# Small attention beside a second attention and two feed-forwards: a fifth work tile, one more step between stages, and normalisations tile by tile

## The chip, the cores and the metric

The kernel runs on one core of a Trainium2 chip. The metric is the device time of one execution in microseconds (us). The kernel before takes 4474.51 us, the median of three runs between 4472.06 and 4476.75.

A core has a matrix engine (TensorE, PE in the profile, with weight loads as PEld), three engines for elementwise work (VectorE or DVE, ScalarE or ACT, GpSimd or POOL), and SyncE (SP), which here only issues DMAs. Each engine works through its own queue strictly in order; an instruction that waits for a semaphore holds up all that stands behind it.

## The reference

Eight sequences of 512 tokens with 256 channels, all in float32, go through four blocks with residuals:

```python
x = x + attention_a(layernorm(x))   # per token: 16 heads of 64 channels, a 64 x 64 causal matrix per head
x = x + ffn(layernorm(x))           # 256 -> 1024 gated, two hidden layers 1024 -> 1024, 1024 -> 256
x = x + attention_b(layernorm(x))   # causal over the 512 tokens, 16 heads of 16 channels
x = x + ffn(layernorm(x))           # the same weights again
```

The first attention is unusual. For each token and head, channel q attends to the channels k <= q of the same token: `softmax_k(Q[q]*K[k]/8)` weighs `V[k]`. There is no contraction for the matrix engine in it; it is elementwise work on 64 x 64 outer products. The feed-forward is `silu(x@w1*s1) * (x@w2*s2)`, then twice `gelu(h@w*s)`, then `h@w3*s3`.

## The kernel before, in words

A batch is one sequence, held as four tiles of 128 tokens by 256 channels in SBUF (`self.x[b]`). `AttentionA` computes the first attention; `after_a` is a Python generator which writes the other three blocks of each batch (`ffn`, `attention_b`, `ffn`). The driver at the end of `fast_path` interleaves the two by hand: under `tc.manual_schedule` the queues of PE, DVE, ACT and POOL hold instructions in the order in which the Python code writes them. The first attention is written step by step; after each of the three `yield`s of a step the driver draws as much from `after_a` as keeps `spent`, the sum of what its `yield`s return, in proportion to `total`. A batch's other blocks are thus written while the first attention works on the next batch, and those of the last batch stand alone at the end.

**The first attention.** A group is one tile of tokens and four heads (`GW` = 256 channels), NG = 4 groups per tile, 16 per batch, 128 in all. The causal triangle is cut into squares of 32, 16, 8, 4, 2 and 1 channels, sorted into four units per group (`units`); a step of the pipeline is one unit. A unit lives in a work tile `w` of 128 x 4096 floats from the pool `wt` (four buffers): half for e = exp(q*k), half for e*v. Its stages are

- `scores` (L718): the products q*k, on POOL from an SBUF copy of q (`kt`) for the first two units, on DVE from q in PSUM for the others;
- `exps` (L731) on ACT;
- `weigh` (L742) on DVE: e*v, with v in PSUM; then for the three large units a DMA that POOL issues (L744) and that adds the second half of the tile onto the first, inside SBUF;
- `fold` (L752) on POOL: for the 32-squares one more halving, which waits for that DMA; for the small squares (L757, L779) additions into `acc`;
- `gather` (L773) on DVE: sums over the last eight columns, then POOL adds them to the rows of `acc` (L779);
- `divide`: a DVE reciprocal (L783) and a POOL product (L784), once per group; `turn_group` (L792) and `project_out` (L801) on PE, and the sum with x on DVE (L808).

In step n, `step` writes the scores of unit n, then `weigh(n - 1)` with its DMA, `fold(n - 2)`, `gather(n - 3)`, and last `exps(n)`. `project` (L686, L693) makes k and q|v of a group two steps ahead with weights `wqv`, `wk` from the pool `wp`, which has two buffers; `load_w` fetches the next group's weights on SP.

**Normalisations.** `stats` takes mean and variance on DVE, the square root on ACT (L518), reciprocal and shift on DVE (L519, L524), for several tiles in one go; `normed` applies them on ACT (L532, L536), PE transposes (L543), ACT copies (L544). Before a feed-forward and before the second attention, three tiles are done together (`begin`) and the fourth later (`norm_last`, `finish`).

**The other blocks.** `later(fn)` puts a piece of code off to the next `flush()`. In `ffn`, `gate` writes silu on ACT (L927) and the product on DVE (L928) right after each other, the rounding to fp32r on ACT (L931) and the remainder on POOL (L932) put off. The hidden layers (L1016) read weights of 1 MB each, whose DMAs POOL issues (L855), 20 per batch with the gates'. Blocks for activations come from the pool `hp` with eight buffers, taken in turn.

Of the kernel before, what the change touches and what calls it, by code (L numbers as in the profile page):

```python
# [16 lines left out]
P = 128  # L17
# [267 lines left out]
def fast_path(ctx: ExitStack, tc: tile.TileContext, k, t, flag):  # L285

    nc = tc.nc
    ident, eps = k.ident, k.eps
# [3 lines left out]
    wp = ctx.enter_context(tc.tile_pool(name="wp", bufs=2))  # L292
# [5 lines left out]
    hp = ctx.enter_context(tc.tile_pool(name="hp", bufs=8))  # L298
# [27 lines left out]
    for g in range(NG):  # L326
        if g < 2:

            wqv = wp.tile([P, DC, 2 * GW], F32, tag="wqv", name=f"wqv_0_{g}")
            wk = wp.tile([P, DC, GW], F32, tag="wk", name=f"wk_0_{g}")  # L330
        else:
            both = block(f"fit_{g}")
            wqv = both[:, : DC * 2 * GW].rearrange("p (c f) -> p c f", c=DC)
            wk = both[:, DC * 2 * GW : DC * 3 * GW].rearrange("p (c f) -> p c f", c=DC)
        nc.sync.dma_start(wqv, wqv_r[:, :, g, :])
        nc.sync.dma_start(wk, wk_r[:, :, g * GW : (g + 1) * GW])
        fitted.append((wqv, wk))
# [171 lines left out]
    def stats(b, xt, part, tiles=range(NT)):  # L509

        i0, i1 = tiles[0], tiles[-1] + 1
        mv = small.tile([P, NT, 2], F32, tag=f"mv_{part}", name="mv", bufs=2)[:, i0:i1]
        for i in tiles:
            st = small.tile([P, 6], F32, tag=f"st_{part}", name="st")
            nc.vector.bn_stats(st, xt[:, i, :])
            nc.vector.bn_aggr(mv[:, i - i0, :], st)
        rstd = small.tile([P, NT], F32, tag=f"rstd_{part}", name="rstd", bufs=2)[:, i0:i1]
        nc.scalar.activation(rstd, mv[:, :, 1], AF.Sqrt, bias=eps)  # L518
        nc.vector.reciprocal(rstd, rstd)  # L519
        if part == "f":  # L520
            shift = small.tile([P, NT], F32, tag="shift", name="shift", bufs=2)[:, i0:i1]
        else:
            shift = means[:, b, 0 if part == "a" else 1, i0:i1]
        nc.vector.scalar_tensor_tensor(shift, mv[:, :, 0], -1.0, rstd, ALU.mult, ALU.mult)  # L524
        return {i: (rstd[:, i - i0 : i - i0 + 1], shift[:, i - i0 : i - i0 + 1]) for i in tiles}

    def normed(xi, rn, part):

        rstd, shift = rn
# [9 lines left out]
    def turned_over(dst, xn, pool):  # L539
# [4 lines left out]
        nc.scalar.copy(dst, pt)  # L544
# [4 lines left out]
    units = (((32, 0, 2),), ((32, 2, 2),), ((16, 0, 4),), ((8, 0, 4), (4, 0, 4), (2, 0, 4), (1, 0, 4)))  # L549
    NU = len(units)  # L550

# [10 lines left out]
    def pieces(w, n, off, nsq, cols):  # L562
# [11 lines left out]
        if n < 16:  # L574
            e, ev = (
                w[:, a * 2048 + off : a * 2048 + off + nsq * n * n].rearrange("p (x i j) -> p x i j", i=n, j=n)
# [22 lines left out]
    class AttentionA:  # L599
# [3 lines left out]
        def __init__(self):  # L603
            self.x = {0: x_first}
            self.rn, self.live = {}, {}
            self.w = {(0, g): fitted[g] for g in range(2)}
            self.wo = {}
            self.load_wo(0, 0)
            self.ready = set()
# [3 lines left out]
            self.steps = len(self.todo) + 11  # L613
# [10 lines left out]
        def load_wo(self, b, g):  # L624
            if b < NB:
                wo = wp.tile([P, GW // P, D], F32, tag="wo", name=f"wo_{b}_{g}", bufs=1)
# [6 lines left out]
        def step(self, n):  # L633
            b, i, g, u = self.at(n)
            if b is not None:
                self.scores(b, i, g, u)
            b, i, g, u = self.at(n + 40)
            if u == 0 and g == 0 and i == 0 and b > 0:
                self.x[b] = load_x(b)
            b, i, g, u = self.at(n + 7)  # L640
            if u == 0 and g == 0 and i == 0:
                self.rn[b] = stats(b, self.x[b], "a")
            b, i, g, u = self.at(n + 4)
            if u == 0 and g == 0:
                self.norm(b, i)
            yield
            b, i, g, u = self.at(n - 1)
            if b is not None:
                self.weigh(b, i, g, u)
            b, i, g, u = self.at(n - 2)  # L650
            if b is not None:
                self.fold(b, i, g, u)
            b, i, g, u = self.at(n + 2)
            if u == 0:
                self.project(b, i, g)
            yield
            b, i, g, u = self.at(n - 3)
            if b is not None:
                self.gather(b, i, g, u)

            b, i, g, u = self.at(n - 4)
            if u == NU - 1:
                self.divide(b, i, g)
            b, i, g, u = self.at(n - 8)
            if u == NU - 1:
                self.turn_group(b, i, g)
            b, i, g, u = self.at(n - 9)
            if u == NU - 1:
                self.project_out(b, i, g)
            yield  # L670
            b, i, g, u = self.at(n)
            if b is not None:
                self.exps(b, i, g, u)

        def norm(self, b, i):
            xnt = lnp.tile([P, DC, P], F32, tag="xnt_a", name=f"xnta_{b}_{i}", bufs=NT)
            turned_over(xnt, normed(self.x[b][:, i, :], self.rn[b][i], "a"), ps_a)
            self.live[b, i] = xnt

        def project(self, b, i, g):  # L680
# [8 lines left out]
            kt = ap_.tile([P, 2, GW], F32, tag="k", name=f"k_{u}")  # L689
            nc.scalar.copy(kt[:, 0], pk)  # L690
            qv = ps_qv.tile([P, 2, GW], F32, tag="qv", name=f"qv_{u}")
            for c in range(DC):
# [6 lines left out]
                )  # L699
            nc.scalar.copy(kt[:, 1], qv[:, 0])  # L700
            acc = ap_.tile([P, 2, GW], F32, tag="acc", name=f"acc_{u}", bufs=4)
            self.live[b, i, g] = (qv, kt, acc)
            if i == 1 and (b, g) != (0, 0):
                self.load_w(b + (g + 1) // NG, (g + 1) % NG)

        def scores(self, b, i, g, n_u):

            qv, kt, acc = self.live[b, i, g]
            w = wt.tile([P, 4096], F32, tag="w", name=f"w_{b}_{i}_{g}_{n_u}")
            self.live[b, i, g, n_u] = w  # L710
            if n_u == 0:
                nc.vector.tensor_tensor(acc[:, 0, :], qv[:, 0, :], kt[:, 0], ALU.mult)
            for n, off, nsq, cols in squares(units[n_u]):

                eng, q = (nc.gpsimd, kt[:, 1]) if n_u < 2 else (nc.vector, qv[:, 0])
                for e, ev, rows, columns in pieces(w, n, off, nsq, cols):
# [3 lines left out]
                    )  # L720

        def exps(self, b, i, g, n_u):
            qv, kt, acc = self.live[b, i, g]
            w = self.live[b, i, g, n_u]
            if n_u == 0:
                nc.scalar.activation(acc[:, 0, :], acc[:, 0, :], AF.Exp, scale=C**-0.5)
            if n_u < 3:
                e = w.rearrange("p (b a r) -> p a b r", a=2, b=units[n_u][0][0] // JB)[:, 0]
            else:
                e = w[:, : sum(nsq * n * n for n, off, nsq, cols in squares(units[n_u]))]  # L730
            nc.scalar.activation(e, e, AF.Exp, scale=C**-0.5)  # L731

        def weigh(self, b, i, g, n_u):


            qv, kt, acc = self.live[b, i, g]
            w = self.live[b, i, g, n_u]
            if n_u == 0:
                nc.vector.tensor_tensor(acc[:, 1, :], acc[:, 0, :], qv[:, 1, :], ALU.mult)
# [3 lines left out]
            if n_u < 3:  # L743
                nc.gpsimd.dma_start(w[:, :2048], w[:, 2048:], accum_op=ALU.add)  # L744

        def fold(self, b, i, g, n_u):

            qv, kt, acc = self.live[b, i, g]
            w = self.live[b, i, g, n_u]
            for n, off, nsq, cols in squares(units[n_u]):  # L750
                if n == 32:
                    nc.gpsimd.tensor_tensor(w[:, :1024], w[:, :1024], w[:, 1024:2048], ALU.add)  # L752
                if n <= 2:
                    both = w.rearrange("p (a f) -> p a f", a=2)[:, :, off : off + nsq * n * n]
                    both = both.rearrange("p a (r j) -> p a r j", j=n)
                    if n == 2:
                        nc.gpsimd.tensor_tensor(both[..., :1], both[..., :1], both[..., 1:], ALU.add)  # L757
                    self.add_rows(acc, n, cols, both[..., 0])

        def gather(self, b, i, g, n_u):  # L760

            qv, kt, acc = self.live[b, i, g]
            w = self.live.pop((b, i, g, n_u))
            for n, off, nsq, cols in squares(units[n_u]):
                if n <= 2:
                    continue
                if n >= 16:
                    both = w[:, : 2 * nsq * n * JB].rearrange("p (a r j) -> p a r j", a=2, j=JB)
                else:
# [569 lines left out]
```

## Time and profile before

| | |
|---|---|
| median of the runs | 4474.51 us |
| profiled execution | 4477.29 us, span 4475.5 us |
| granted TensorE clock, mean | 0.806 |
| busy, PE / DVE / ACT / POOL | 66% / 78% / 54% / 66% of the span |
| DMA queues: POOL's, SP's | 56.3%, 6.3% of 16 engines |
| activation table loads on ACT | 408, 1283 ns each |
| work DMA (L744) | 384, 1 MB each, 7.2 us from issue to landing |

How to read it: a group's line names the line of the kernel, engine, operation, output and inputs with shape, count, then busy time, mean ns of one, and the idle time of the engine just before it with what ended that. Busy time leaves out instructions that issue DMAs. A wait is listed as waiter, waited-for, us in total, times, longest.

### The profile page before, as it was taken

How to read it: one execution, taken by the hardware profiler on the slowest of the kernel's cores; microseconds unless marked ns; L12 is line 12 of the kernel's file. 1: busy time of each engine (PE TensorE's matmuls, PEld its weight loads, DVE VectorE, ACT ScalarE, POOL GpSimd, SP SyncE). 2: the span in 40 equal slices, each digit the busy share in tenths (PEclk: the TensorE clock that was granted, in tenths of full speed). 3: DMA queues.
4: the chain of work that ended last, by engine and by line, in shares of the span. 5: the costliest groups of instructions: out<-in, count | busy, mean ns of one | idle time of the engine just before them, and what ended most of it. 6: DMA issues, size and time to landing. Idle time of an engine off the chain costs nothing. (4 is left out here: it accounts for less than half of the span.)

```text
span 4475.5 us, 37073 instructions
## 1 busy us (share of the span) xinstructions
PE 2959.5 (66%) x11880; PEld 2017.9 (45%) x11880; DVE 3511.3 (78%) x4113; ACT 2422.0 (54%) x3068; POOL 2962.6 (66%) x2634
## 2 busy tenths in 40 slices
PE   3322277567865777757875678657777568756998
PEld 2111154245633555335642456335553356425757
DVE  5988877888888888878878788888888788787205
ACT  3333365565754765556654666547655566546332
POOL 6777776766776776767767667667767677676201
PEclk6555588788987889878987889778898789878999
DMA  7555566657755767647765577557676477655514
GB/s 234 124 123 119 123 163 168 124 140 178 192 125 111 181 165 176 134 112 177 178 168 124 139 177 198 119 111 182 161 178 133 110 180 172 168 115 135 180 43 147
DMA packets 118364, 670.24 MB, mean 150 GB/s; under 512 B 12672, under 2 KB 31883, under 8 KB 43536
## 3 DMA queue, kind: packets, MB, share of 16 engines
q0 software_dynamic: 78336, 570.46, 56.3%
q1 hardware_dynamic: 39824, 97.32, 6.3%
q8 instruction: 96, 1.57, 0.1%
q14 instruction: 108, 0.88, 0.1%
HBM read 255.12 MB, written 9.96 MB: 59 GB/s over the span
## 5 line engine op out<-in xcount | busy, mean ns | idle before, releaser
L742 DVE TENSOR_TENSOR w<-w,qv 128x1024 f32<-128x1024 f32 (+3 forms) x1280 | 1198.7, 985 | 443.5 <-ACT w L731 443.5
L731 ACT ACTIVATE w<-w 128x2048 f32<-128x2048 f32 (+1 forms) x512 | 966.0, 1887 | 842.0 <-POOL w L718 560.8
L1016 PE MATMUL ph<-h,hidden 128*128 128x512 f32 x4096 | 1095.3, 424 | 158.4 <-POOL h L932 90.4
L773 DVE TENSOR_REDUCE red<-w 128x128 f32<-128x1024 f32 (+2 forms) x640 | 1036.6, 1636 | 23.9 <-POOL w L752 19.1
L718 POOL TENSOR_TENSOR w<-k 128x1024 f32<-128x1024 f32 x512 | 1036.2, 2136 | 7.6 <-ACT k L700 7.4
L1016 PEld LDWEIGHTS ph<-h,hidden 128*128 128x128 f32 x4096 | 819.7, 203 | 386.9 <-POOL h L932 113.7
L744 POOL DMA_DIRECT2D w<-w x384 | 334.8, 872 | 979.1 <-DVE w L742 331.4
L752 POOL TENSOR_TENSOR w<-w 128x1024 f32<-128x1024 f32 x256 | 664.1, 2594 | 64.6 <-DMA w<-w 64.2
L718 DVE TENSOR_TENSOR w<-qv,k 128x1024 f32<-128x1024 f32 (+3 forms) x768 | 601.5, 838 | 6.9
L779 POOL TENSOR_TENSOR acc<-acc,red 128x256 f32<-128x256 f32 (+1 forms) x640 | 473.1, 739 | 139.5 <-DVE red L773 121.0
L948 PE MATMUL pw<-xnt,gate 128*128 128x512 f32 (+2 forms) x1152 | 328.7, 439 | 166.8 <-ACT silu L927 84.6
L543 PE MATMUL ps_ln<-ident,xn 128*128 128x128 f32 x256 | 76.5, 415 | 488.7 <-ACT xn L536 330.6
L1126 PE MATMUL pyb<-eb,vb 128*32 128x512 f32 (+3 forms) x1024 | 219.6, 525 | 255.7 <-ACT eb L1121 255.5
L948 PEld LDWEIGHTS pw<-xnt,gate 128*128 128x128 f32 x1152 | 236.6, 225 | 244.9 <-ACT silu L927 101.8
L686 PE MATMUL pk<-wk,xnta 128*128 128x256 f32 x512 | 191.6, 512 | 196.6 <-DVE x L808 195.2
L693 PE MATMUL qv<-wqv,xnta 128*128 128x512 f32 x512 | 288.0, 692 | 0.0
L543 PEld LDWEIGHTS ps_ln<-ident,xn 128*128 128x128 f32 x256 | 37.3, 193 | 529.7 <-ACT xn L536 353.7
L1041 PE MATMUL pof<-w,h 128*128 128x256 f32 x1024 | 244.9, 399 | 12.5 <-ACT h L981 12.5
L981 ACT ACTIVATE h<-ph,s_sb 128x512 fp32r<-128x512 f32 (+1 forms) x256 | 172.2, 688 | 129.7 <-PE ph L1016 128.4
L1126 PEld LDWEIGHTS pyb<-eb,vb 128*32 128x32 f32 x1024 | 66.2, 117 | 362.2 <-ACT eb L1121 336.5
L686 PEld LDWEIGHTS pk<-wk,xnta 128*128 128x128 f32 x512 | 124.1, 258 | 231.4 <-DVE x L808 206.3
L1041 PEld LDWEIGHTS pof<-w,h 128*128 128x128 f32 x1024 | 204.4, 202 | 48.0 <-ACT h L981 17.3
(130 smaller groups left out, 4196.5 us busy)
## 6 DMA issues: line engine op xcount, KB each, us to landing
w<-w POOLq DMA_DIRECT2D x384, 1024.0 KB, 7.2
hidden<-in_h POOLq DMA_DIRECT2D x128, 1024.0 KB, 6.6
gate<-in_w12p POOLq DMA_DIRECT2D x32, 1024.0 KB, 5.7
w<-w_d SPq DMA_DIRECT2D x16, 1024.0 KB
wqv<-wqv_d SPq DMA_DIRECT2D x30, 512.0 KB, 3.1
wo<-in_wo SPq DMA_DIRECT2D x32, 256.0 KB, 6.6
wbqk<-wbqk_d SPq DMA_DIRECT2D x8, 1024.0 KB
w<-in_h SPq DMA_DIRECT2D x8, 1024.0 KB, 8.5
```

The lines of the kernel that those rows point to most:

```text
L686: nc.tensor.matmul(pk, xnt[:, c, :], wk[:, c, :], start=(c == 0), stop=(c == DC - 1))
L693: nc.tensor.matmul(qv.rearrange("p j f -> p (j f)"), xnt[:, c, :], wqv[:, c, :], start=(c == 0), stop=(c == DC - 1),)
L718: eng.tensor_tensor(e, rows(q).to_broadcast(shape), columns(kt[:, 0]).to_broadcast(shape), ALU.mult)
L731: nc.scalar.activation(e, e, AF.Exp, scale=C**-0.5)
L742: nc.vector.tensor_tensor(ev, e, columns(qv[:, 1]).to_broadcast(list(e.shape)), ALU.mult)
L744: nc.gpsimd.dma_start(w[:, :2048], w[:, 2048:], accum_op=ALU.add)
L752: nc.gpsimd.tensor_tensor(w[:, :1024], w[:, :1024], w[:, 1024:2048], ALU.add)
L773: nc.vector.tensor_reduce(red, both, AX.X, ALU.add)
L779: nc.gpsimd.tensor_tensor(rows, rows, part.rearrange("p a (x i) -> p a x i", i=n), ALU.add)
L948: nc.tensor.matmul(pj[:, toks], w[:, m % 4, j, c, :], xs[:, p, c, toks], start=(p == 0 and c == 0), stop=(p == 1 and c == DC - 1),)
L1016: nc.tensor.matmul(pss[j], w[:, j, c, :], h_in(p, c), start=(p == 0 and c == 0), stop=(p == 1 and c == MC - 1),)
L1041: nc.tensor.matmul(po, h(0, c)[:, i * P : (i + 1) * P], w3[:, c, :], start=(c == 0), stop=(c == MC - 1))
```

## The change

It has five parts.

1. *The first attention's pipeline.* The units are reordered, 32, 16, 32 and small; POOL does the scores of the first and third. The small unit gets a work tile of its own (`ws`, one buffer, two times 1920 floats), so with the four `w` there are five. `exps` moves to the next step, `weigh` to n - 2, the DMA becomes a stage of its own (`halve`) between the two halves of POOL's scores, `fold` is at n - 3, `gather` at n - 4 (small unit: n - 3), POOL's additions one part after the gather. Projections, copies, transposes and additions to x are split and spread over the steps.
2. *Normalisations.* `stats` becomes `moments` on DVE and `scales` on POOL, with the power -0.5 of variance + eps in place of square root and reciprocal. `Normed` works tile by tile, each link put off to a later `flush`, and the blocks that read it wait (`nx.wait`) until enough tiles are written.
3. *Other blocks.* In `gate` the product is put off by one flush; the additions to x in `attention_b` too.
4. *Buffers.* The pool `wp` has one buffer instead of two, `load_w` comes at the group's last projection; `hp` has seven instead of eight, with hidden activations in pairs of chunks.
5. *The driver.* The loop begins two steps earlier, `total` is 304.8 instead of 299.4, the pipeline is one step shorter at its end; the weights of groups 1 to 3 are fitted during the first steps.

```diff
-    wp = ctx.enter_context(tc.tile_pool(name="wp", bufs=2))
+    wp = ctx.enter_context(tc.tile_pool(name="wp", bufs=1))
...
-    hp = ctx.enter_context(tc.tile_pool(name="hp", bufs=8))
+    hp = ctx.enter_context(tc.tile_pool(name="hp", bufs=7))
...
-        nc.scalar.activation(rstd, mv[:, :, 1], AF.Sqrt, bias=eps)
-        nc.vector.reciprocal(rstd, rstd)
...
-        nc.vector.scalar_tensor_tensor(shift, mv[:, :, 0], -1.0, rstd, ALU.mult, ALU.mult)
...
+    def scales(mv, rstd, shift):
+        nc.gpsimd.tensor_scalar(rstd, mv[:, :, 1], EPS, None, ALU.add)
+        nc.gpsimd.tensor_tensor(rstd, rstd, k.power[:, : rstd.shape[-1]], ALU.pow)
+        nc.gpsimd.tensor_tensor(shift, mv[:, :, 0], rstd, ALU.mult)
+        nc.gpsimd.tensor_scalar(shift, shift, -1.0, None, ALU.mult)
...
-    units = (((32, 0, 2),), ((32, 2, 2),), ((16, 0, 4),), ((8, 0, 4), (4, 0, 4), (2, 0, 4), (1, 0, 4)))
+    units = (((32, 0, 2),), ((16, 0, 4),), ((32, 2, 2),), ((8, 0, 4), (4, 0, 4), (2, 0, 4), (1, 0, 4)))
...
+    SMALL = 1920
...
         def step(self, n):
-            b, i, g, u = self.at(n)
-            if b is not None:
-                self.scores(b, i, g, u)
...
+            before = self.at(n - 2)
+            if before[0] is not None:
+                self.weigh(*before)
+            unit = self.at(n)
+            on_pool = unit[3] in (0, 2)
+            if on_pool:
+                half = self.scores(*unit)
+                next(half)
+            if before[0] is not None:
+                self.halve(*before)
+            if on_pool:
+                next(half, None)
...
+            if self.at(n - 1)[0] is not None:
+                self.exps(*self.at(n - 1))
+            yield
+            if unit[0] is not None and not on_pool:
+                for _ in self.scores(*unit):
+                    pass
+            for args in self.sums:
+                self.add_rows(*args)
+            self.sums = []
+            b, i, g, u = self.at(n - 3)
+            if u in (0, 2):
+                self.fold(b, i, g, u)
...
+            yield
+            b, i, g, u = self.at(n - 4)
+            if u in (0, 1, 2):
+                self.gather(b, i, g, u)
+            b, i, g, u = self.at(n - 3)
+            if u == NU - 1:
+                self.gather(b, i, g, u)
+            b, i, g, u = self.at(n + 3)
+            if u == 0:
+                self.project(b, i, g)
...
-            if i == 1 and (b, g) != (0, 0):
+            if i == NT - 1:
                 self.load_w(b + (g + 1) // NG, (g + 1) % NG)
...
-            w = wt.tile([P, 4096], F32, tag="w", name=f"w_{b}_{i}_{g}_{n_u}")
+            if n_u < NU - 1:
+                w = wt.tile([P, 4096], F32, tag="w", name=f"w_{b}_{i}_{g}_{n_u}")
+            else:
+                w = wt.tile([P, 2 * SMALL], F32, tag="ws", name=f"ws_{b}_{i}_{g}", bufs=1)
...
-                eng, q = (nc.gpsimd, kt[:, 1]) if n_u < 2 else (nc.vector, qv[:, 0])
+            eng, q = (nc.gpsimd, kt[:, 1]) if n_u in (0, 2) else (nc.vector, qv[:, 0])
...
+        def tile(self, i):
+            mv = small.tile([P, 1, 2], F32, tag="mv", name="mv")
...
+            moments(self.xt[:, i, :], mv[:, 0, :])
+            def scale():
+                scales(mv, rstd, shift)
+                later(normalise)
+            def normalise():
+                xn = normed(self.xt[:, i, :], rstd, shift, self.part)
+                later(lambda: turn_tile(xn))
...
+            later(scale)
+
+        def wait(self, tiles):
+            while self.done < tiles:
+                flush()
+                yield 0.8
...
+            def times():
+                nc.vector.scalar_tensor_tensor(x, p2, s_sb[:, 1, m : m + 1], x, ALU.mult, ALU.mult)
+                later(high)
...
-    total = 299.4
+    total = 304.8
...
-        for n in range(-7, a.steps):
+        for n in range(-9, a.steps):
```

## The prediction

> **What bounds the kernel now.** I read the page's totals first, then the waits, then the first attention running alone, then one batch cut at each reciprocal (one per group of four units). The page, and the waits of VectorE:
>
> ```profile
> PE 2959.5 (66%) x11880; PEld 2017.9 (45%) x11880; DVE 3511.3 (78%) x4113; ACT 2422.0 (54%) x3068; POOL 2962.6 (66%) x2634
> ...
> L744 POOL DMA_DIRECT2D w<-w x384 | 334.8, 872 | 979.1 <-DVE w L742 331.4
> ...
> w<-w POOLq DMA_DIRECT2D x384, 1024.0 KB, 7.2
> ```
>
> ```profile
> DVE w L742 <- ACT w L731: 443.5, 143, 6.2
> DVE silu L928 <- ACT silu L927: 158.4, 64, 5.3
> ```
>
> No engine is full. VectorE is the fullest, and it stands mostly before the weighting, waiting for an exponential. GpSimd's 66% leaves out the issuing of DMAs. From about 110 to 545 us the first attention runs alone; VectorE and GpSimd there, in the timeline:
>
> ```profile
> 352.93 0.41 DVE L739 TENSOR_TENSOR acc<-acc,qv 128x256 f32<-128x256 f32 x1
> 356.90 2.35 DVE L742 TENSOR_TENSOR w<-w,qv 128x1024 f32<-128x1024 f32 x2 [3.56 <-ACT w L731]
> ```
>
> ```profile
> 375.20 2.64 POOL L752 TENSOR_TENSOR w<-w 128x1024 f32<-128x1024 f32 x1
> 377.51 0.74 POOL L779 TENSOR_TENSOR acc<-acc,red 128x128 f32<-128x128 f32 x1
> 377.91 1.01 POOL L784 TENSOR_TENSOR acc<-acc 128x256 f32<-128x256 f32 x1
> 378.60 4.13 POOL L718 TENSOR_TENSOR w<-k 128x1024 f32<-128x1024 f32 x2
> ...
> 387.60 0.86 POOL L744 DMA_DIRECT2D w<-w  x1 [0.66 <-DVE w L742]
> 388.21 0.91 POOL L757 TENSOR_TENSOR w<-w 128x256 f32<-128x256 f32 x1
> ```
>
> ```profile
> DMA to landing us min/median/max: 6.9/7.0/7.6
> ```
>
> Reciprocals stand 27.82 us apart (347.28, 375.11, 402.92). VectorE has 24.19 us of work in that, plus one stall of 3.56: GpSimd's scores, the exponential and the weighting follow each other without slack. The last line is the accumulating DMA in this stretch: it lands 7.0 us after its issue, 7.6 at most.
>
> One later batch takes 522.95 us (753.83 to 1276.78), VectorE busy for 433.0. Its groups by stage (us, length, busy PE, PEld, DVE, ACT, POOL, clock, DMA share, GB/s):
>
> ```profile
> 781.67:809.47 27.80, 18.73 (x111) 8.01 (x108) 24.19 (x26) 15.02 (x26) 20.87 (x19) 0.81 0.66 144
> 932.29:976.97 44.68, 32.57 (x107) 24.51 (x107) 32.04 (x45) 32.89 (x37) 32.18 (x30) 0.77 0.57 142
> 1205.33:1237.06 31.73, 29.33 (x121) 22.91 (x120) 24.29 (x26) 18.89 (x19) 20.94 (x19) 0.95 0.92 235
> ```
>
> ```profile
> DMA to landing us min/median/max: 7.0/8.1/12.6
> ```
>
> First, a group beside the second attention's scores: nothing lost against running alone. There are five such, 140.2 us. Second, a group beside a gate; the five at normalisations and gates take 205.4 us, VectorE busy 155.7. Third, a group beside the hidden layers: six, 177.4 us, with DMA engines up to 92% busy; the last line is the accumulating DMA from 1147 to 1237 us, landing in 8.1, at worst 12.6.
>
> **What the Trainium skill says.** "Perfetto Trace Analysis", per-instruction lifecycle: the profiled end of a GpSimd-issued DMA is the end of descriptor generation, not of the data. The trace agrees: 0.87 us of L744 against 7.0 to landing. "DMA: Bandwidth & Descriptors", issuing engines are not separate queues: all DMAs interleave on the same 16 engines. Agreed: the landing grows where weights load. "ScalarE: Activation LUTs", what a table load costs: 1283 ns at each change of set. The trace has exactly that, 1283. "GPSIMD Engine Reference", 3.1: a two-input operation costs GpSimd about twice VectorE's time. Here 128x1024 takes 1.9 to 2.1 us against 1.2.
>
> **The change, part by part.**
>
> *One more step.* The weighting moves from n-1 to n-2, its DMA between the two halves of the scores, the fold to n-3, the gather to n-4; units become 32, 16, 32, small, so that GpSimd's scores (u 0 and 2) alternate with VectorE's. This removes the 3.56 stall: the exponential of u=0 now has the whole next step. VectorE's work stays 24.2. What is late next is GpSimd's fold, which waits for the DMA. GpSimd's queue per group, start to start from the stretch above: scores 4 x 1.91, issues 3 x 0.61, folds 2 x 2.31, small squares 1.00 + 1.74, additions 2 x 0.41 + 0.73 + 1.5, division 0.69: 20.6. In the new order between the DMA of u=2 and its fold lie its own 0.61, half a score 1.91, division 0.69, addition 0.41: 3.6 us; landing in 7.0 leaves a stall of 3.4. For u=0: 0.61 + 1.91 + 0.73 + 0.61 + 0.41 + 1.5 = 5.8, stall 1.2. Before, a fold had a whole step, 7.5 to 8.6 us, and hardly waited. So GpSimd takes 20.6 + 4.6 = 25.2, more than VectorE: about 2.6 us saved per group running alone. Behind the waiting fold are the next scores; their exponential has some 5 us of slack.
>
> *Normalisations.* Square root, reciprocal and shift leave ScalarE and VectorE: about 5 us of VectorE per batch, and 408 table loads become some 304, 104 x 1.283 = 133 us of ScalarE, which isn't full, so nothing directly. GpSimd gets 13 x 4 tiny dependent operations per batch. The trace has no power. An addition of 128x128 costs 0.45 alone, 128x1024 1.95: 0.23 fixed, 0.3 to 0.35 with a dependence. Lower end 4 x 0.3 = 1.2 us per tile; upper end, a power of several us, 6. I take 1.6, as the power must cost something: 12 x 1.6 = 19 us per batch, all in the five normalisation and gate groups. In exchange each link is put off by a flush, so the engines no longer stand in the chain.
>
> *Gate, additions, copies put off.* VectorE's wait for silu (158.4 in all) should mostly go.
>
> *Single buffers of qkv weights.* The load is now issued after the group's last projection, four steps (about 29 us) ahead of need; landings are 3.1 and 6.3 us. Waits ahead of it on SP are for earlier TensorE work. Nothing; uncovered it would cost up to 9 us x 31. Seven hidden blocks instead of eight: each reuse follows a reader that is already done. Nothing; up to 5 us per layer if not. "q and v in PSUM" is what L718 and L742 read already.
>
> *A batch.* Beside scores: landing 7.4 there, GpSimd 26.0 a group, five are 130. Hidden layers: 20.6 + 1.1 other work + 2.7 weight issues x 0.62 + stalls at a landing of 8.1 of 4.5 + 2.3, less 1.8 filled by the added work: 28.3; the DMA engines' own work is about 25 us per group (share x length), 88% of that, so landings will grow: I take 29, six are 174. Normalisations and gates: GpSimd busy 127.9, DMA issues 12, powers 19, remaining stalls 6, waits for the feed-forward's own chain 5: 170 (VectorE would need 150.7). Sum 474 instead of 523.
>
> *The sum.* Before, in the span of 4475.5: first reciprocal 91.6; 16 groups alone to 544.5; 111 groups to 4154.1, at 32.5; last batch 321, TensorE busy 295 of it. After: 91.6 + 16 x 25.2 = 495; 111 x 474/16 = 3288; tail 321 (three norm chains lose 1.3 and gain 1.6 each: nothing). Total 4104. The profiled execution took 4477.3, span 4475.5, median of the runs 4474.5, so span and time are the same within 2 us: 4105.
>
> **Rivals.**
>
> *VectorE alone bounds (20%).* POOL's stalls fall where VectorE is busy, or the landing gets shorter. Batch 433 - 5 + 2% = 436; alone 24.7: 487 + 3025 + 321 = 3833. For it: VectorE is the fullest engine now. Against: the two gaps of 3.6 and 5.8 us, which are in the instruction order.
>
> *The second chain keeps its delays (21%).* TensorE and ScalarE run in order through feed-forward and second attention; put-off links only wait elsewhere, a GpSimd that lags blocks ScalarE at a normalisation, and the hidden layers get slower with DMA. Gain only running alone and beside scores: 16 x 2.6 + 6.9 x 10 = 112: 4363. For it: TensorE is busy for 29.3 of 31.7 us in the hidden group shown. Against: the DVE waits named above are in the gate groups.
>
> *The power is dear (9%), slower.* GpSimd sets the pace in the normalisation groups, so each us beyond 1.6 costs 99 tiles x 1 us. The gain of 370 is gone at 5.4 us per tile. At 7: 4105 + 535 = 4640. Only the absence of any power in the trace speaks for it; other small operations cost 0.1 to 0.7.
>
> *No effect (2%)*: the fold's wait takes all that the exponential's gave. Running alone that needs a landing of 9.6 us instead of 7.0.
>
> **How the numbers follow.** Forecast 48%: 4105, own range 4010 to 4220. A measurement tells about 0.2% from no change, 9 us. Range: down to 3850 for most of the first rival, up to 4370 for the second; outside remain the slow case and some of the first. Faster 0.89, same 0.02, slower 0.09.
>
> **What would show it.** Right: reciprocals 25 to 25.5 us apart between 150 and 480 us; the wait of w L742 for the exponential below 150 us in all; the fold waiting for its DMA over 300 us in all (64 before), the largest wait on GpSimd; table loads near 304; gate groups 33 to 36 us; hidden groups not faster than 28. Wrong: a VectorE over 92% busy before the tail (first rival), gate groups still near 40 (second), the power's row over 2 us each (third), reciprocals alone still near 27.8.

## The result and the profile after

The changed kernel takes 4235.1 us (median of four runs, 4227.3 to 4244.9), against 4475.6 before: a ratio of 0.946 (0.944 to 0.949). The gain is 240 us where the forecast said 370; the time lies inside the stated range and 15 us outside the forecast's own. The profiled execution has a span of 4228.3 us.

The page's totals after the change, the issue of the work tile's DMA (L790, L744 before), and the DMA's median from issue to landing:

```profile
PE 2912.1 (69%) x11880; PEld 1983.7 (47%) x11880; DVE 3455.7 (82%) x4001; ACT 2265.4 (54%) x2911; POOL 3099.8 (73%) x3051
...
L790 POOL DMA_DIRECT2D w<-w x384 | 354.0, 922 | 208.1 <-DVE w L784 104.5
...
w<-w POOLq DMA_DIRECT2D x384, 1024.0 KB, 7.8
```

VectorE and GpSimd are busy for a larger share of a shorter span. VectorE's own work hardly shrank (3511 to 3456 us): what went is waiting. The waits of the kernel after:

```profile
PE pta L844 <- POOL acc L836: 660.1, 110, 19.5
ACT w L774 <- POOL w L760: 652.8, 177, 18.2
POOL w L795 <- DMA w<-w: 476.5, 148, 12.5
...
DVE w L784 <- ACT w L774: 83.8, 25, 5.3
...
DVE ws L784 <- ACT ws L774: 49.8, 8, 18.5
```

The weighting's wait for the exponential fell from 443.5 to 133.6 us: the 443.5 before covered all four units of a group, and the kernel after lists the small unit's tile `ws` apart. GpSimd's fold (L795) now waits 476.5 us for its DMA, and TensorE (L844, transposition of the first attention's result) 660.1 us for GpSimd's division (L836). The first was forecast. The second was not.

GpSimd in the stretch where the first attention runs alone, in the timeline (start, length, what it is, and in brackets the idle time ahead of it):

```profile
383.48 2.35 POOL L795 TENSOR_TENSOR w<-w 128x1024 f32<-128x1024 f32 x1 [0.61 <-DMA w<-w]
...
387.68 0.87 POOL L790 DMA_DIRECT2D w<-w  x1
388.28 2.24 POOL L760 TENSOR_TENSOR w<-k 128x1024 f32<-128x1024 f32 x1
390.20 1.00 POOL L836 TENSOR_TENSOR acc<-acc 128x256 f32<-128x256 f32 x1
390.89 0.72 POOL L828 TENSOR_TENSOR acc<-acc,red 128x128 f32<-128x128 f32 x1
394.67 2.36 POOL L795 TENSOR_TENSOR w<-w 128x1024 f32<-128x1024 f32 x1 [3.06 <-DMA w<-w]
```

The first line is the fold of u=0, the last that of u=2 (u counts the units of a group from 0). Between the issue of the DMA of u=2 and its fold stand half a score, a division and an addition; the fold starts 6.99 us after the issue, as it lands, having waited 3.06 us. Forecast were 3.4, and 1.2 for u=0, which waits 0.61. Over the 14 groups running alone the two waits are 3.1 and 0.6 us in the mean.

Below, stages are means over six batches (groups 17 to 112, sixteen reciprocals of L832 each; the prediction had one batch of them), "alone" is over the 3rd to the 17th reciprocal; "scores" are the five groups of a batch beside the second attention's scores, "gates" the five at normalisations and gates, "hidden" the six beside the hidden layers.

| | alone, per group | scores | gates | hidden | batch | last reciprocal to end |
|---|---|---|---|---|---|---|
| before | 28.0 | 140.3 | 203.3 | 178.4 | 522.0 | 321 |
| forecast | 25.2 | 130 | 170 | 174 | 474 | 321 |
| after | 25.0 | 141.4 | 172.6 | 178.9 | 492.8 | 305.5 |

The whole gain of a batch lies in the gate groups; scores and hidden groups gained nothing. One group of each stage, with the columns us, length, busy PE, PEld, DVE, ACT, POOL, clock, DMA share, GB/s:

```profile
785.67:813.95 28.28, 16.35 (x98) 7.45 (x100) 24.03 (x27) 14.70 (x26) 20.83 (x19) 0.74 0.55 112
842.84:877.66 34.82, 20.74 (x79) 15.94 (x79) 31.84 (x52) 16.18 (x22) 25.90 (x39) 0.75 0.48 99
1131.69:1166.41 34.72, 27.24 (x108) 21.64 (x106) 25.02 (x29) 17.93 (x17) 21.62 (x19) 0.90 0.85 222
```

In the gate group VectorE works for 31.8 of 34.8 us. In the other two it works for 24 to 25 us as before and stands for the rest: 4.3 beside the scores, 9.7 beside the hidden layers.

### The profile page after: what moved, and what is told of

It reads as the page before. It is cut to its first block, busy times and chain, and to the rows that moved or that the text cites. A ratio compares the mean times of both kernels' runs of the same rounds, so it can differ in the third digit from the quotient of the medians.

```text
span 4228.3 us, 37111 instructions
## 1 busy us (share of the span) xinstructions
PE 2912.1 (69%) x11880; PEld 1983.7 (47%) x11880; DVE 3455.7 (82%) x4001; ACT 2265.4 (54%) x2911; POOL 3099.8 (73%) x3051
## 4 chain that ended last, share of the span: by engine, by line
POOL 36%; DVE 16%; issue 16%; PE 15%; ACT 8%; DMA 8%; SPq 0%; POOLq 0%; ACTq 0%; DVEq 0%
POOL w L760 12%; POOL w L795 8%; DMA w<-w 7%; DVE red L821 6%; POOL acc L828 5%; DVE w L784 5%; PE ph L1095 4%; POOL w L790 4%; ACT w L774 3%; PE qv L725 2%; POOL acc L836 2%; PE pqkb L1141 1%; DVE ws L760 1%; POOL h L1011 1%; PE pw L1027 1%
## 5 line engine op out<-in xcount | busy, mean ns | idle before, releaser
L760 POOL TENSOR_TENSOR w<-k 128x1024 f32<-128x1024 f32 x512 | 1077.5, 2105 | 10.9 <-ACT k L741 7.8
L774 ACT ACTIVATE w<-w 128x2048 f32<-128x2048 f32 x384 | 735.0, 1917 | 653.4 <-POOL w L760 652.8
L795 POOL TENSOR_TENSOR w<-w 128x1024 f32<-128x1024 f32 x256 | 610.2, 2384 | 559.4 <-DMA w<-w 476.5
L784 DVE TENSOR_TENSOR w<-w,qv 128x1024 f32<-128x1024 f32 x768 | 899.2, 1211 | 85.3 <-ACT w L774 83.8
L821 DVE TENSOR_REDUCE red<-w 128x128 f32<-128x1024 f32 (+1 forms) x384 | 598.9, 1560 | 178.5 <-POOL w L795 120.4
L844 PE MATMUL pta<-ident,acc 128*128 128x128 f32 x256 | 75.3, 390 | 660.1 <-POOL acc L836 660.1
L790 POOL DMA_DIRECT2D w<-w x384 | 354.0, 922 | 208.1 <-DVE w L784 104.5
L821 DVE TENSOR_REDUCE red<-ws 128x256 f32<-128x2048 f32 (+1 forms) x256 | 435.4, 1742 | 0.0
L844 PEld LDWEIGHTS pta<-ident,acc 128*128 128x128 f32 x256 | 34.2, 180 | 703.6 <-POOL acc L836 698.7
L784 DVE TENSOR_TENSOR ws<-ws,qv 128x1024 f32<-128x1024 f32 (+3 forms) x512 | 298.6, 644 | 49.8 <-ACT ws L774 49.8
L760 DVE TENSOR_TENSOR w<-qv,k 128x1024 f32<-128x1024 f32 x256 | 299.9, 1212 | 0.0
L760 DVE TENSOR_TENSOR ws<-qv,k 128x1024 f32<-128x1024 f32 (+3 forms) x512 | 299.6, 646 | 0.0
L774 ACT ACTIVATE ws<-ws 128x1920 f32<-128x1920 f32 x128 | 231.6, 1810 | 30.7 <-DVE ws L760 30.0
```

The costliest lines, as they stand in the source:

```text
L760: eng.tensor_tensor(e, rows(q).to_broadcast(shape), columns(kt[:, 0]).to_broadcast(shape), ALU.mult)
L784: nc.vector.tensor_tensor(ev, e, columns(qv[:, 1]).to_broadcast(list(e.shape)), ALU.mult)
L821: nc.vector.tensor_reduce(red, self.columns_of(w, n, off, nsq), AX.X, ALU.add)
```

## Experiments

Two theories for the missing 130 us. **Theory 1:** beside the scores, TensorE stands in its queue before the transposition, for GpSimd's division; the second attention's matmuls stand behind it, then ScalarE, then the weighting. **Theory 2:** the fold's wait for the accumulating DMA sets the pace in all stages. Further runs take the parts of the change one by one. All kernels start from the one after unless said otherwise; times are medians, ratios are against the kernel before.

### The transposition one step later

```diff
-            b, i, g, u = self.at(n - 6)
-            if u == NU - 1:
-                self.turn_group(b, i, g)
...
             yield
+            b, i, g, u = self.at(n - 7)
+            if u == NU - 1:
+                self.turn_group(b, i, g)
...
-            b, i, g, u = self.at(n - 6)
-            if u == NU - 1:
-                nc.scalar.copy(self.live["att"], self.live.pop("pta"))
...
             yield
+            b, i, g, u = self.at(n - 7)
+            if u == NU - 1:
+                nc.scalar.copy(self.live["att"], self.live.pop("pta"))
```

> The transposition of the first attention's result (L844) and its copy are put one step later, so that TensorE no longer waits in order for GpSimd's division (L836). Theory 1 (that wait holds up the second attention's matmuls, then ScalarE, then the weighting): the wait PE pta L844 <- POOL acc falls from 660 to under 150 us, groups beside the second attention's scores go from 28.4 to about 26 us, the whole to about 4155 (28.4 less 26, five groups, seven batches: 80 us). Theory 2 (the accumulating DMA and GpSimd's fold set the pace everywhere; TensorE's wait is only where idle time shows): within 15 us of 4235.

4182.0 us, ratio 0.935 (0.933 to 0.936): 53 us faster than after. TensorE's wait for the division, 660.1 us in the kernel after, is gone from the trace. Scores fall from 141.4 to 134.8, gates (171.9) and hidden groups (177.9) stay within about 1 us, alone 24.99 stays. In the chain, first in the kernel after, beside the scores:

```profile
790.66 2.34 DVE L760 TENSOR_TENSOR w<-qv,k 128x1024 f32<-128x1024 f32 x2
790.78 1.00 POOL L836 TENSOR_TENSOR acc<-acc 128x256 f32<-128x256 f32 x1
...
791.83 0.69 PE L844 MATMUL pta<-ident,acc 128*128 128x128 f32 x2 [8.47 <-POOL acc L836]
...
800.79 0.59 ACT L1217 COPY ytb<-pyb 128x512 f32<-128x512 f32 x1 [5.14 <-PE pyb L1208]
...
804.49 1.96 ACT L774 ACTIVATE w<-w 128x2048 f32<-128x2048 f32 x1
...
806.49 2.35 DVE L784 TENSOR_TENSOR w<-w,qv 128x1024 f32<-128x1024 f32 x2 [4.25 <-ACT w L774]
```

VectorE's scores are ready at 793.0; their exponential (L774) starts at 804.49, because ScalarE stands in order before a copy for the second attention (L1217), which waits for TensorE, which had waited 8.47 us for the division. The weighting waits 4.25. With the transposition later, the same scores and their exponential:

```profile
790.75 2.35 DVE L760 TENSOR_TENSOR w<-qv,k 128x1024 f32<-128x1024 f32 x2
...
798.88 1.97 ACT L774 ACTIVATE w<-w 128x2048 f32<-128x2048 f32 x1
```

The exponential starts 5.8 us after the end of the scores instead of 11.5. Beside the scores, the wait of the large units' weighting for the exponential falls from 9.6 to 1.8 us a batch, and the stage by 6.5. Theory 1 is right beside the scores and hardly elsewhere: the gain is 53 us of the 80 it reckoned with.

### The small squares ahead of the fold

```diff
-            b, i, g, u = self.at(n - 3)
-            if u in (0, 2):
-                self.fold(b, i, g, u)
             b, i, g, u = self.at(n - 2)
             if u == NU - 1:
                 self.small_squares(b, i, g)
+            b, i, g, u = self.at(n - 3)
+            if u in (0, 2):
+                self.fold(b, i, g, u)
```

> GpSimd does the small squares ahead of the fold of u=2, which so gets 2.7 us more for its DMA to land. Theory 2 (the fold's wait for the DMA sets the pace): the wait POOL w L795 <- DMA falls from 476 to under 200 us, groups running alone from 24.9 to about 24.2, which is VectorE's own work, and groups beside hidden layers from 29.9 to about 28.5: the whole to about 4180. Theory 1 (the order on TensorE and ScalarE): running alone the same 24.2, but the other stages stay, and the whole is 4215 to 4230.

4099.1 us, ratio 0.916 (0.915 to 0.918): 136 us faster, more than either theory said. The fold's wait:

```profile
POOL w L795 <- DMA w<-w: 217.3, 96, 8.5
```

Running alone 24.17 a group, which is VectorE's work; gates 165.0 (from 172.6), hidden groups 169.8 (from 178.9), scores 140.2 (from 141.4). The order of two blocks on GpSimd, with not one instruction less, is worth over half of what the whole change brought. Stage by stage, the fold's wait for the DMA and the time fell by these amounts in a batch:

| us per batch | scores | gates | hidden |
|---|---|---|---|
| less waiting of the fold | 8.8 | 5.5 | 14.8 |
| shorter stage | 1.2 | 7.6 | 9.1 |

So theory 2 is right running alone and beside the hidden layers, where VectorE's reductions, which wait for the DMA or the fold, stand 7.7 us less. Beside the scores it is wrong. At the gates the gain is larger than the wait that went, so the new order brings something else there too; what, was not traced.

### Half of each hidden weight's load

```diff
+                if name == "hidden" and self.n < 181:
+                    eng.dma_start(w[:, : HB // 2], src[:, : HB // 2])
...
-                            w[:, j, c, :],
+                            w[:, j if checked else 0, c, :],
```

> Leaves out half of each 1 MB load of a hidden weight (the products use the other half twice, so TensorE has the same work). If the weights' loads delay the accumulating DMA and so GpSimd's fold in the hidden groups: its landing there falls from medians of 8 to 10 us to about 7.2, the six groups from 179 to about 168 us per batch, the whole to about 4160. If order and work set those groups: landing may fall, but the whole stays within 15 us of 4235.

4180.1 us, ratio 0.933 (0.931 to 0.934): 55 us faster. Hidden groups 171.2, from 178.9; scores (142.2) and gates (172.3) stay. The work DMA's landing in the two hidden stretches of one batch falls from medians of 9.1 and 8.0 us to 8.2 and 7.7, the longest from 18.6 to 15.1. Over the six batches the fold's wait in this stage falls from 37.8 to 28.3 us a batch, and VectorE's reductions stand 7.4 us less, about the 7.7 that the stage gained. GpSimd's issues of the weights' loads are no shorter (0.76 and 0.75 us each), so the gain does not come from there. So the weights' loads do delay the fold, by the longest landings more than by the median.

### The added step alone undone, the alternation alone undone

```diff
-            before = self.at(n - 2)
+            before = self.at(n - 1)
...
-            if self.at(n - 1)[0] is not None:
-                self.exps(*self.at(n - 1))
...
+            if unit[0] is not None:
+                self.exps(*unit)
             yield
```

`exps` moves to the end of the step; fold and small squares go to n - 2 and n - 1, the gathers to n - 3 and n - 2. Division, transposition and all behind them stay.

> Undoes the added step alone: exponentials at the end of their own step, weighting one step after the scores, its DMA, fold and gather one step earlier too; units stay 32, 16, 32, small, and all else is as after. If the added step is what removed the stall before the weighting: groups running alone go from 24.9 back to 27 to 28 us, the wait DVE w L784 <- ACT from 84 to over 300 us; if it also carries the batches, these get 35 us longer and the whole is about 4500; if the batches' gain is that of the normalisations and gates, the whole is 4270 to 4330. If the alternation of the units alone did it: alone below 25.5, the whole within 30 us of 4235.

4688.7 us, ratio 1.047 (1.046 to 1.049): slower than before. Alone 30.1 us a group where 27 to 28 were expected, a miss: without the step the new order is worse than the old. The wait of the large units' weighting for the exponential is 776.7 us, against 83.8 after.

```diff
-    units = (((32, 0, 2),), ((16, 0, 4),), ((32, 2, 2),), ((8, 0, 4), (4, 0, 4), (2, 0, 4), (1, 0, 4)))
+    units = (((32, 0, 2),), ((32, 2, 2),), ((16, 0, 4),), ((8, 0, 4), (4, 0, 4), (2, 0, 4), (1, 0, 4)))
...
-            on_pool = unit[3] in (0, 2)
+            on_pool = unit[3] in (0, 1)
```

The folds and the engine of the scores go with the units.

> Undoes the alternation alone: units again 32, 32, 16, small, GpSimd's scores in the first two steps of a group, VectorE's in the last two; the added step and all else as after. If the alternation is a needed part: GpSimd stands in a row of two scores and VectorE in another, groups running alone go from 25.0 to 26.5 or more and the whole to 4330 or more. If the added step does it alone: 24.2 to 25.2 alone, the whole between 4150 and 4250.

4422.7 us, ratio 0.987 (0.985 to 0.989). Alone 27.2 us a group.

| us per group, running alone | units in a row | units alternating |
|---|---|---|
| weighting one step after the scores | 28.0 (before) | 30.1 |
| weighting two steps after the scores | 27.2 | 25.0 (after) |

With the new order, the step is worth 5.1 us a group; with the step, the alternation is worth 2.2. The upper left cell is not as cleanly a neighbour: before, GpSimd issues the DMA behind its scores and not between their halves, and the small unit has no tile of its own. So the 30.1 are not the price of the alternation by itself. What costs there is seen in that kernel's timeline:

```profile
319.65 2.34 DVE L784 TENSOR_TENSOR w<-w,qv 128x1024 f32<-128x1024 f32 x2
...
322.54 0.87 POOL L790 DMA_DIRECT2D w<-w  x1 [5.44 <-DVE w L784]
323.15 2.25 POOL L760 TENSOR_TENSOR w<-k 128x1024 f32<-128x1024 f32 x1
...
325.43 1.91 ACT L774 ACTIVATE w<-w 128x2048 f32<-128x2048 f32 x1 [5.86 <-POOL w L760]
...
327.38 2.35 DVE L784 TENSOR_TENSOR w<-w,qv 128x1024 f32<-128x1024 f32 x2 [5.38 <-ACT w L774]
```

The DMA's issue stands between the two halves of GpSimd's scores. It waits for the weighting; the second half waits behind it; that half's exponential and weighting follow. So the two engines wait for each other by turns. With one more step the weighting in question is further back, and over the whole kernel after, GpSimd's wait at L790 is 104.5 us instead of 473.9. What holds the kernel with the units in a row was not traced further; GpSimd's wait for the weighting at L790 is 460.4 us there against 104.5.

### Only the second chain changed

The kernel after, with `AttentionA`, its units, buffers and driver loop from before (there `stats` on ScalarE and VectorE too); the core of it:

```diff
-            before = self.at(n - 2)
-            if before[0] is not None:
-                self.weigh(*before)
...
+            b, i, g, u = self.at(n)
+            if b is not None:
+                self.scores(b, i, g, u)
...
+            b, i, g, u = self.at(n - 1)
+            if b is not None:
+                self.weigh(b, i, g, u)
```

So only the tile-by-tile normalisations with the power (in the second chain), the put-off gates and additions, the hidden activations in pairs of chunks and the driver's `total` are new.

> The kernel after with the first attention, its weights' buffers and its steps of before; only the second chain is new (normalisations tile by tile with the power, gates and additions put off). If the gain at normalisations and gates comes from these: those five groups go from 203 to 170 to 178 us, scores (140) and hidden groups (178) stay as before, the whole 4240 to 4300. If it comes from the slack that the added step gives the first attention: those groups stay above 195, the whole 4420 to 4480.

4326.4 us, ratio 0.966 (0.964 to 0.968). Gates 177.3, scores 143.9, hidden groups 180.0. It lies between the two expectations: the second chain's edits bring 26 of the 31 us that a batch gains at the gates and lose 5 in the other two stages. Of the 240 us, 149 come with them, and the other 91 when the first attention's part is added, with its buffers and the driver's loop. The first attention's part without the second chain's was not run, so what it would bring by itself stays open.

### The power undone

```diff
-        nc.gpsimd.tensor_scalar(rstd, mv[:, :, 1], EPS, None, ALU.add)
-        nc.gpsimd.tensor_tensor(rstd, rstd, k.power[:, : rstd.shape[-1]], ALU.pow)
-        nc.gpsimd.tensor_tensor(shift, mv[:, :, 0], rstd, ALU.mult)
-        nc.gpsimd.tensor_scalar(shift, shift, -1.0, None, ALU.mult)
+        nc.scalar.activation(rstd, mv[:, :, 1], AF.Sqrt, bias=k.eps)
+        nc.vector.reciprocal(rstd, rstd)
+        nc.vector.scalar_tensor_tensor(shift, mv[:, :, 0], -1.0, rstd, ALU.mult, ALU.mult)
```

(`mv`, `rstd` and `shift` of a tile have four buffers instead of three here.)

> Undoes the power alone: square root on ScalarE, reciprocal and shift on VectorE, tile by tile as after. The prediction's reckoning (1.6 us of GpSimd per tile bought for 5 us of VectorE per batch, table loads worth nothing): table loads from 304 back to some 410 or more, and the whole between 4150 (GpSimd's time in the normalisation groups counts in full: 12 x 1.25 us x 7 batches less 35) and 4250. If the table loads do cost (some 110 more of 1.28 us on ScalarE, in front of an exponential that the weighting needs): 4290 to 4370.

4307.1 us, ratio 0.962 (0.961 to 0.964): 72 us slower than after, all of it at the gates (182.3 from 172.6). Table loads rise from 307 to 423. But VectorE's busy time also rises, by 112 us, for operations on one number per partition. In the timeline:

```profile
1021.47 0.16 DVE L519 SCALAR_TENSOR_TENSOR shift<-mv,rstd 128x1 f32<-128x1 f32 x1
...
1031.69 2.22 POOL L759 TENSOR_TENSOR w<-k 128x1024 f32<-128x1024 f32 x1
...
1032.60 2.02 DVE L519 SCALAR_TENSOR_TENSOR shift<-mv,rstd 128x1 f32<-128x1 f32 x1
1033.61 0.98 POOL L827 TENSOR_TENSOR acc<-acc,red 128x256 f32<-128x256 f32 x1
```

The shift takes 0.16 us where GpSimd is idle. It takes 2.02 where it starts during an operation of GpSimd that another one follows; it ends at 1034.62, 0.03 us after the second of them. Of this operation's 104 executions 49 took over 0.5 us, and each of these ended within 0.1 us of the end of an operation of GpSimd. A further kernel has the same, but for single tiles with the reciprocal as a scalar operand, so that only one tensor in SBUF goes in:

```diff
-        nc.vector.scalar_tensor_tensor(shift, mv[:, :, 0], -1.0, rstd, ALU.mult, ALU.mult)
+        nc.vector.tensor_scalar(shift, mv[:, :, 0], rstd, -1.0, ALU.mult, ALU.mult)
```

> As the run without the power (4307 us), but VectorE forms each tile's shift with one tensor input and the reciprocal as a scalar operand, instead of two tensor inputs in SBUF. If VectorE's two-input operation waits for GpSimd's operations to end (it took 0.16 us beside an idle GpSimd and up to 3.5 beside a busy one): the shift takes under 0.3 us each, VectorE's busy time falls by 70 to 90 us, the whole to 4230 to 4265. If the table loads and the waits for ScalarE's square root are what costs: VectorE's busy time may fall, but the whole stays at 4290 or more.

4268.6 us, ratio 0.953 (0.951 to 0.955), between the two expectations. The shift now takes 0.21 us each time, and VectorE is busy for 77 us less. So of the 72 us, 39 are VectorE waiting for GpSimd inside an operation, and 33 are left for the square root's way over ScalarE, net of GpSimd's four operations saved: table loads stay at 423, and VectorE waits 99 us for its results.

### The start's loads in their own memory

```diff
-        sk = block("sk").rearrange("p (c f) -> p c f", c=DC)
+        sk = hwp.tile([P, HB], F32, tag="hw", name="sk").rearrange("p (c f) -> p c f", c=DC)
```

The two blocks of `sqv` likewise.

> The loads sqv and sk of the first column group's fit get their own memory (the buffers of the hidden weights, not used by then), so they wait for no block that the later weights hold. If that wait is what put the second reciprocal at 137 us: it comes at 115 to 120 us, and the whole at 4215. If something else in the start (the fit's own matmuls, or VectorE's share of it) is next in line: the second reciprocal stays above 130 and the whole within 8 us of 4235.

4217.4 us, ratio 0.942 (0.940 to 0.943): 18 us faster. The second reciprocal comes at 123.6 instead of 137.1 us, somewhat later than expected, and the 17th at 496.9 instead of 510.7. In the kernel after SP issues the load of `sk` only at 86.84 us (58.97 before; 76.80 with this edit), and ScalarE stands waiting for it. By the code it comes behind blocks of the later weights, now that there are seven and the fit of the second group takes one of them:

```profile
103.46 1.06 ACT L374 ACTIVATE sk<-sk 128x1024 f32<-128x1024 f32 x1 [18.59 <-DMA sk<-in_wqkv]
```

### The three together, and one more for the fold

The three edits shown above in one kernel:

> The later transposition, the earlier small squares and the start's loads together. If the three act in different stages, as their runs alone suggest (53 us beside the scores, 136 where GpSimd's fold waits, 17 in the start), the gains add: 4235 - 53 - 136 - 17 = 4029, within 15. If they share a limit (VectorE, or GpSimd's other waits), 4060 to 4085.

4050.3 us, ratio 0.904 (0.902 to 0.906): 185 us faster than after. The gains alone (53, 136, 18) add up to 207, so most of them add. Alone 24.15, scores 133.4, gates 165.5, hidden 170.8. The totals and the chain of work that ended last:

```profile
PE 2922.4 (72%) x11880; PEld 1964.4 (49%) x11880; DVE 3445.5 (85%) x4001; ACT 2260.2 (56%) x2911; POOL 3100.0 (77%) x3051
...
DVE 39%; POOL 24%; PE 15%; issue 10%; ACT 9%; DMA 2%; SPq 0%; POOLq 0%; ACTq 0%; DVEq 0%
```

In the kernel after that chain was 36% on GpSimd and 8% on DMAs, with VectorE at 16%. Now VectorE leads. This is the fastest kernel here. One more edit puts the folds between the halves of GpSimd's next scores:

```diff
                 self.halve(*before)
+            b, i, g, u = self.at(n - 4)
+            if u in (0, 2):
+                self.fold(b, i, g, u)
             if on_pool:
                 next(half, None)
...
-            b, i, g, u = self.at(n - 3)
-            if u in (0, 2):
-                self.fold(b, i, g, u)
```

> On top of the three edits together (4050): each fold is put off to between the two halves of GpSimd's next scores, so its DMA has some 2 to 4 us more to land. If what is left of the fold's wait (246 us) still sets the pace in the hidden and normalisation groups: that wait falls below 100 us, the hidden groups from 171 to about 164 us per batch, the whole to 3980 to 4010. If VectorE and the second chain's order set it now: the wait falls, but the whole stays within 15 us of 4050; if the later fold makes VectorE's reduction wait for it, 4060 or more.

4497.3 us, ratio 1.004 (1.003 to 1.006): all is lost again, and a group running alone takes 30.0 us. The fold no longer waits for the DMA (245.7 us ahead of this edit), but its reader waits for the fold:

```profile
DVE red L821 <- POOL w L795: 652.9, 244, 13.6
...
POOL w L760 <- DVE red L821: 233.0, 114, 4.2
```

VectorE's reduction waits for the late fold, and GpSimd's next scores wait for that reduction to free one of the four work tiles: one tile goes round among all stages, and a later fold holds it longer. The fold now also stands ahead of the second half of those scores, and ScalarE's wait for them grows from 637 to 789 us; the two effects were not taken apart.

## Why the prediction was right or wrong

**One more step: right.** Alone 25.0 against 25.2, the stall of the fold at u=2 3.1 against 3.4, at u=0 0.6 against 1.2, the weighting's wait 134 us with the small units (forecast under 150), the fold's wait 476 (over 300, and the largest on GpSimd). GpSimd's own work and other waits are 0.6 us a group more than the 20.6 reckoned, so the total is closer than its terms. What the forecast did not see: the step and the alternation need each other (30.1 without the one, 27.2 without the other), and the place of the small squares behind the fold, which made most of that stall, cost 136 us over the whole kernel.

**Normalisations and gates: right in size, in part by luck.** 172.6 against 170 for the five groups, table loads 307 against 304. The power takes 0.57 us and the four operations 1.21 us busy, 1.56 from the start of one tile's to the next's; 1.6 was taken. "Nothing directly" for what leaves ScalarE and VectorE was too low: it is worth 72 us. It was hidden in the sum, as the stage was reckoned from GpSimd's queue and VectorE's work and not from the old waits. GpSimd's busy time there came as forecast (146.8 us a batch, 127.9 + 19). But that it sets the pace is not borne out: without the power it works 18 us a batch less there, and the stage is 9.7 longer. That the second chain gained is by itself shown: 149 us.

**A batch, "Beside scores: … GpSimd 26.0 a group, five are 130": the step that failed.** Measured are 141.4. The sum counted GpSimd's queue and gave the exponential slack. It did not ask what stands behind TensorE's transposition when GpSimd comes late. The later transposition brings back 6.5 of the 11.4 us; with all three edits the stage is at 133.4. There VectorE still stands 9.9 us a batch: 6.8 before a weighting, for its exponential, and 3.0 before a reduction, for the fold. Why these come late was not traced.

**"Hidden layers … I take 29, six are 174": mis-sized.** Measured 178.9. The landing was put at 8.1 us, with some growth for load; medians were 8.0 to 10.2 in the stretches looked at, and single landings took up to 18.6. Over the six batches the median in this stage went from 7.7 before the change to 9.6 after; why it grew by so much is open. Both a longer gap before the fold (169.8) and lighter loads (171.2) bring the stage below 174.

**The sum.** Seventeenth reciprocal 510.7 against 495: the start was taken as unchanged, and one load is 28 us later; mending it brings back 13.8. The 111 groups 3412 against 3288: the two stages above, and 2.6 a batch at the gates. The tail 305.5 against 321: with only the second chain changed it is 317.7, so most of the gain comes with the first attention; it was not traced. Together +16, +124, -16: 4228 against 4104.

**The rivals.** VectorE alone as the bound gave 3833; even with three mended places 4050 is left. "The second chain keeps its delays" put the gain running alone and beside the scores (10 us a batch) and none at the gates: in the batches it came the other way round. What it said of TensorE and ScalarE working in order, so that a lagging GpSimd holds up others, did happen: ScalarE waits 147 us in all for GpSimd at normalisations, and TensorE 660 at the transposition, which the rival did not name. A dear power is out: 1.6 us per tile. A single edit of this order leads to slower than before, the weighting one step nearer (4.7%), and another back to where it was, the folds later; neither by the mechanism that the slow rival named. The landing of 9.6 us under "no effect" does not follow from the prediction's own queue: stalls of the landing less 3.6 and less 5.8, on 20.6 us of work, reach 27.8 at 8.3.

## What to carry to other kernels

When one more step of distance removes a wait, list for every engine in the new order what stands between each wait and its releaser, and what is queued behind the waiter, on the matrix engine too: two blocks swapped on GpSimd, a transposition put off and a load's memory were worth 185 us, on top of the 240 of the change itself. Judge order and distance together, since each can be useless or harmful alone. A buffer that goes round through all stages limits how far a late stage can be put off.

## What the runs showed that was not expected

VectorE's operation with two inputs in SBUF took 0.16 us beside an idle GpSimd and up to 3.5 us beside a busy one, ending as GpSimd's operation ended; with one tensor input it took 0.21 us each time. The Trainium skill has this ("SBUF — State Buffer", section "SBUF: two separate sides"): VectorE with two SBUF inputs and GpSimd take a shared pair of ports as an exclusive lock, and the loser blocks for the whole instruction. The trace agrees, and adds that GpSimd's next operation got in as well: the 2.02 us span two of them. VectorE's large operations read q or v from PSUM and so have only one input in SBUF, and they showed no such wait: none of the 128x1024 products of L760 and L784 in the kernel after took over 1.23 us.

The same 1 MB accumulating DMA inside SBUF landed after 7.0 us alone and up to 18.6 us beside loads of hidden weights, while the median in those stretches moved by only 1 to 3 us. The same loads at half the size brought the longest down to 15.1.
